# Causal attention and a recurrence taken in pieces of four batches amid the context attention before them

## The chip, the core and the metric

The kernel runs on one NeuronCore of a Trainium2 chip, in fp32, as one program with hand-placed work on TensorE (PE in the profile; its weight loads, which can overlap its matmuls, are PEld), VectorE (DVE), ScalarE (ACT) and GpSimd (POOL). SyncE (SP) issues most transfers. The metric is the device time of one execution in microseconds (us); a median of several is compared with a median of several.

## The reference

A model of four layers works on `x`, 16 batches of 64 tokens with 256 features (1024 tokens in all). Each layer adds three blocks to `x`: an attention over a context of 16 x 1024 keys with 192 features, a token mixer, and an FFN. Each block is fed a layer norm of `x`.

```python
x = x + _L0_xattn_ref(_layernorm(x), ctx_768, ctx_768, ...)
x = x + _L0_attn_ref(_layernorm(x), ...)
x = x + _L0_ffn_ref(_layernorm(x), ...)
...
x = x + _L2_xattn_ref(_layernorm(x), ctx_768, ...)
x = x + _L2_attn_ref(_layernorm(x), ...)
x = x + _L2_ffn_ref(_layernorm(x), ...)
...
```

Three of them matter here. The mixer of layer 0 is a causal attention with 16 heads of 16 features within each batch's 64 tokens, with queries and keys RMS-normed over all 256 features:

```python
qkv = jnp.einsum('bglc,cd->bgld', xg, w_qkv)
q, k, v = jnp.split(qkv, 3, axis=-1)
q = rmsnorm(q, ln_w)
k = rmsnorm(k, ln_w)
...
att = jnp.einsum('bghqd,bghkd->bghqk', q, k) * scale
att = jax.nn.softmax(jnp.where(causal, att, -jnp.finfo(att.dtype).max), axis=-1)
y = jnp.einsum('bghqk,bghkd->bghqd', att, v)
...
return jnp.einsum('btc,cd->btd', y, w_proj)
```

The FFN of layer 0 is a mixture of 8 experts: a gate's softmax chooses two per token, and a shared SwiGLU with 384 hidden features is added for all tokens. The mixer of layer 2 is a linear recurrence over a batch's 64 tokens with 128 complex states:

```python
Bu = jnp.einsum('hd,bld->blh', B_norm, x)
_, h = jax.lax.associative_scan(_binop, (Lam, Bu), axis=1)   # h_t = Lam * h_(t-1) + Bu_t
y = jnp.einsum('oh,blh->blo', C, h).real + D * x
```

All these blocks but the mixture's routing work on each batch by itself, so once the context attention has written the `x` of some batches, their mixer can begin.

## The kernel before, in words

`x` stays on chip as `xs`, 8 tiles of 128 tokens (two batches each; NT = 8). `LAYERS` names the blocks; `run` calls them in turn, each with its own SBUF pool (`lp`) and PSUM pools (`lps`, and the shared `misc` buffers, two in most blocks). Weights come through `ring`, two slots of 7296 columns; `slot` takes the next, `load` issues one weight's DMA on SP, and `pack` hands a block its weights and starts the loads of the block after it.

**Order.** Each engine executes its instructions in the order in which they were built. By default a scheduler orders PE's; within `manual_schedule` PE's order is the order in which the program text is run. A tile's PSUM or SBUF buffer is given out again when its last reader is done, so a producer may wait for the reader of an older tile.

**Layer 0's context attention** (`L0_xattn`, L269). The key projection is folded into the queries (`qp`), so scores come directly from the fetched context. `staggered` runs `first` (L293) for step i and then `second` (L307) for step i - 1, eight steps of two batches. `first` fetches the context of two batches (`fetch_ctx`, two layouts, 3.07 MB a step in all), makes scores of 128 queries x 1024 keys in PSUM tile `sc` (two buffers) and takes maximum (DVE) and exponential (ACT) in `exp_rows` (L218). `second` transposes probabilities (`keys_first`, L226; one copy out of PSUM by DVE, one by ACT), averages the context, transposes the average, projects it and adds it to `xs`.

**The causal attention** (`L0_attn`, L544). It starts with a DMA that writes zeros to `hs`, the 3.4 MB array in HBM that holds the experts' tokens. `norm_x` norms all 1024 tokens and transposes them to `hT`. A first loop over the 8 tiles computes q, k and v, scales q and k by their RMS (`nhalf` is the exponent of a POOL power), transposes them and spreads them by heads into `qs` and `kT`. The second loop takes groups of four batches and half the heads of each as steps: scores of 64x64 blocks (L596), mask, maximum, exponential, sums (DVE, POOL, ACT); transposes (`turned`, L629), averages (L642), division by the sums (`shares`, `weighed`, L658 to L669) and projection (L686). Two or three steps are in flight at a time, in an order written out by hand.

**Layer 0's FFN** (`L0_ffn`, L993). `norm_x`, then `gate_logits`, `gate_softmax` (L926; its first DVE instruction is `g_mx`), `two_largest`, `ranks`, `blocks`, `slots_of` compute on DVE to which row of `hs` each token goes. `scatter` (L1104) writes the tokens there with 16 indirect DMAs on POOL. Expert weights are gathered by indirect DMAs (`L0_block`, L966). `swiglu` (L973) computes the shared part in two halves of 512 tokens: hidden features from PSUM tiles tagged `gu`, silu on ACT, a product on DVE into `hid`, output product, add to `xs`. PE gets it after the gate. Then 23 blocks of 128 rows: read tokens from `hs` (`hb`, on SP), gated product, output to `ys`.

**Layer 2** (`heads64`, L358, then `L2_attn`, L1433). `heads64` is an attention with 8 heads of 64 features, also used in layer 3, with PE's order by hand. In its loop it calls `breathe()` four times a step and `finished(i)` when the tile i of `xs` is complete. In layer 3 these hooks run pieces of that layer's mixer (`state_space`, whose `go` is the hook at L1760) between the pieces of attention; in layer 2 they do nothing. `with_keys` (L409) makes the folded queries `qp` in PSUM tiles that DVE copies out. `L2_attn` norms all tokens, then takes two halves of 512 tokens: two products with B, a rotation by cos and sin, two scans, a rotation back (14 elementwise instructions shared by DVE and POOL), the products with C, and an add to `xs`; `later_steps` makes the mask that restarts the scan at each batch.

Of the kernel before, what the change touches and what calls it, by code (L numbers as in the profile page):

```python
# [19 lines left out]
T = B * S  # L20
# [13 lines left out]
    "L0_xattn", "L0_attn", "L0_ffn", "L1_xattn", "L1_attn", "L1_ffn",  # L34
    "L2_xattn", "L2_attn", "L2_ffn", "L3",
# [5 lines left out]
class Net:  # L41
# [220 lines left out]
    def pack_L0_xattn(self):  # L262
        self.slot()
        return (
            self.load("L0x_WqT"), self.load("L0x_Wk"),
            self.load_ctx_weights("L0x_WvT", "L0x_bv"),
        )

    def L0_xattn(self):  # L269
        nc = self.nc  # L270
        wq, wk, wv = self.pack(ahead=False)
        self.more_ctx(self.lp)
        self.norm_x()
        hT = self.hT
        qT = self.lp.tile([128, 2, T], F32, name="qT")
        for half in range(2):
            cols = bass.ts(half, 512)
            for o in range(2):
                ps = self.misc([128, 512])
                self.mm(ps, [(wq[:, c, o * 128 : (o + 1) * 128], hT[:, c, cols]) for c in range(2)])  # L280
                nc.vector.tensor_scalar(
                    qT[:, o, cols], ps, self.col("L0x_bq", o), D**-0.5, ALU.add, ALU.mult
                )
        qp = self.lp.tile([HC + 1, 2, T], F32, name="qp")
        for half in range(2):
            cols = bass.ts(half, 512)
            for ch in range(2):
                rows = HC + ch
                ps = self.misc([rows, 512])
                self.mm(ps, [(wk[:, o, ch * HC : ch * HC + rows], qT[:, o, cols]) for o in range(2)])  # L290
                self.evict(qp[:rows, ch, cols], ps)

        def first(i):  # L293
            ctx = [self.fetch_ctx(2 * i + par) for par in range(2)]
            sc = self.lps.tile([128, KEYS], F32, tag="sc", bufs=2, name="sc")
            for kh in range(2):
                keys = bass.ts(kh, 512)
                for ch in range(2):
                    for par in range(2):
                        b = 2 * i + par  # L300
                        nc.tensor.matmul(
                            sc[64 * par : 64 * par + 64, keys], qp[: HC + ch, ch, b * S : (b + 1) * S],
                            ctx[par][0][: HC + ch, ch, keys], start=ch == 0, stop=ch == 1,
                        )
            return ctx, self.exp_rows(sc)

        def second(i, got):  # L307
            ctx, p = got
            pT = self.keys_first(p)
            o = self.misc([128, CD + 1])  # L310
            for t in range(NK):
                for par in range(2):
                    nc.tensor.matmul(
                        o[64 * par : 64 * par + 64, :], pT[:, t, 64 * par : 64 * par + 64], ctx[par][1][:, t, :],
                        start=t == 0, stop=t == NK - 1,
                    )
            on = self.averages(o, CD + 1)
            ps = self.misc([128, 2, 128])
            nc.tensor.transpose(ps[:HC, 0, :], on[:, :HC], self.ident)
            nc.tensor.transpose(ps[: HC + 1, 1, :], on[:, HC:], self.ident)  # L320
            onT = self.lp.tile([HC + 1, 2, 128], F32, tag="onT", bufs=2, name="onT")
            nc.vector.tensor_copy(onT[:HC, 0, :], ps[:HC, 0, :])
            nc.scalar.copy(onT[: HC + 1, 1, :], ps[: HC + 1, 1, :])
            po = self.misc([128, D])
            self.mm(po, [(onT[: HC + ch, ch, :], wv[: HC + ch, ch, :]) for ch in range(2)])
            self.add_to_x(i, po)


        self.staggered(first, second, range(NT))
        self.start_pack(self.at)  # L330
        del self.ctxT[2:], self.ctx[2:]
# [26 lines left out]
    def heads64(self, large=None, breathe=lambda: None, finished=lambda i: None):  # L358
# [111 lines left out]
        with self.tc.manual_schedule(engines={mybir.EngineType.PE}):  # L470
# [8 lines left out]
            for k in range(len(steps) + 2):  # L479
# [12 lines left out]
                breathe()  # L492
# [5 lines left out]
                breathe()  # L498
                if one is not None:
                    one["pT"].append(self.keys_first(one["p"][1]))  # L500
                breathe()
# [3 lines left out]
                breathe()  # L505
# [16 lines left out]
    def pair_masks(self):  # L522
# [3 lines left out]
        of = self.lp.tile([8, 2, 128], I32, name="of")  # L526
        nc.gpsimd.iota(of, pattern=[[128, 2], [1, 128]], base=0, channel_multiplier=0)
        nc.vector.tensor_scalar(of, of, 4, None, ALU.logical_shift_right)
        head = self.lp.tile([8, 2, 128], F32, name="head")
        nc.vector.tensor_copy(head, of)  # L530
        mine = self.lp.tile([8, 2], F32, name="mine")
        sel = self.lp.tile([8, 2, 2, 128], F32, name="sel")
# [3 lines left out]
        own = self.lp.tile([128, 2], F32, name="own")  # L536
# [3 lines left out]
    def pack_L0_attn(self):  # L540
        self.slot()
        return self.load("L0a_wqkv"), self.load("L0a_wproj")

    def L0_attn(self):  # L544
        nc = self.nc
        wqkv, wproj = self.pack()

        self.nc.sync.dma_start(
            self.hs.rearrange("(n p) d -> p n d", p=128),
            self.zero.unsqueeze(1).to_broadcast([128, SLOTS // 128, D]),  # L550
        )
        self.norm_x()
        hT = self.hT

        lw = self.lp.tile([128, 2, 2], F32, name="lw")
        for c in range(2):
            nc.vector.tensor_scalar(lw[:, c, :], self.pair4, self.col("L0a_lnw", c), None, ALU.mult)
        qs = self.lp.tile([128, 2, B, 2, S], F32, name="qs")
        kT = self.lp.tile([128, 2, T], F32, name="kT")
        v = self.lp.tile([128, NT, D], F32, name="v")  # L560
        sel, own = self.pair_masks()
        for i in range(NT):
            cols = slice(i * 128, (i + 1) * 128)
            ps = self.misc([128, 2, D])
            self.mm(ps.rearrange("p a b -> p (a b)"), [(hT[:, c, cols], wqkv[:, c, :512]) for c in range(2)])
            sq = self.lp.tile([128, D], F32, tag="sq", bufs=2, name="sq")
            ss = self.small.tile([128, 2], F32, name="ss")
            for j in range(2):
                nc.scalar.activation(sq, ps[:, j, :], AF.Square, accum_out=ss[:, j : j + 1])
            nc.vector.tensor_scalar(ss, ss, 1.0 / D, 1e-6, ALU.mult, ALU.add)  # L570
            rr = self.small.tile([128, 2], F32, name="rr")
            nc.gpsimd.tensor_tensor(rr, ss, self.nhalf.to_broadcast([128, 2]), ALU.pow)
            qk = self.lp.tile([128, 2, D], F32, tag="qk", bufs=2, name="qk")
            for j in range(2):
                nc.vector.tensor_scalar(qk[:, j, :], ps[:, j, :], rr[:, j : j + 1], None, ALU.mult)
            pv = self.misc([128, D])
            self.mm(pv, [(hT[:, c, cols], wqkv[:, c, 512:]) for c in range(2)])
            nc.scalar.copy(v[:, i, :], pv)
            pt = self.lps.tile([128, 2, 2, 128], F32, tag="t", bufs=2, name="pt")
            for j in range(2):  # L580
                for c in range(2):
                    nc.tensor.transpose(pt[:, j, c, :], qk[:, j, c * 128 : (c + 1) * 128], self.ident)
            for c in range(2):
                for h in range(2):
                    nc.vector.tensor_scalar(
                        qs[:, c, 2 * i : 2 * i + 2, h, :], pt[:, 0, c, :].rearrange("p (b s) -> p b s", s=S),
                        lw[:, c, h : h + 1], None, ALU.mult,
                    )
                nc.vector.tensor_scalar(kT[:, c, cols], pt[:, 1, c, :], self.col("L0a_lnw", c), None, ALU.mult)

        sums = {}

        def first(x):  # L596
            g, jp = x
            if not jp:
                sums[g] = self.lp.tile([128, 4, 8], F32, tag="sums", bufs=2, name="sums")
            sc = [self.lps.tile([128, 2, 4, S], F32, tag="sc", bufs=2, name="sc") for _ in range(2)]  # L600
            for c in range(2):
                for bl in range(4):
                    b = 4 * g + bl
                    for u in range(2):
                        rows = slice(64 * jp + 32 * u, 64 * jp + 32 * u + 32)
                        self.mm(
                            sc[u][:, c, bl, :],
                            [(qs[rows, c, b].rearrange("p h q -> p (h q)"), kT[rows, c, b * S : (b + 1) * S])],
                        )
            ps = []  # L610
            for u in range(2):
# [12 lines left out]
                ps.append(p)  # L624
            return ps

        os = {}

        def turned(x, p):  # L629
            pT = []  # L630
# [1454 lines left out]
```

## Time and profile before

| | |
|---|---|
| median of 3 runs | 3145.02 us (3143.34 to 3146.72) |
| profiled execution | 3149.47 us, its span 3147.7 us |
| mean granted clock of TensorE | 0.928 |
| busy: PE, DVE, ACT, POOL | 2778.8 us (88%), 1476.1 (47%), 995.2 (32%), 309.9 (10%) |
| instructions | 42539 |
| moved by DMA | 273.17 MB, 87 GB/s on average |

The stages that the change touches, by the trace, in us from the span's start:

| stage | from | to |
|---|---|---|
| layer 0: context attention (first scores to last output) | 31.5 | 145.3 |
| layer 0: causal attention, norm, gate logits | 146 | 286.8 |
| layer 0: routing, shared FFN, scatters | 286.8 | 334.5 |
| layer 0: expert blocks | 334.5 | 546 |
| layer 2: context attention | 1430 | 1943.6 |
| layer 2: recurrence (last product) | 1943.6 | 1982.5 |

The rows of a page's second part cut the span in 40 slices of 78.7 us. A digit is the busy share in tenths (9 is 90% or more); PEclk is the clock that TensorE was granted, in tenths of full speed. In finer windows that clock takes two values in this trace, 1.00 and 0.50, and a matmul record takes twice as long at the lower. The profile's PE records are modelled at their ends, so a PE that counts as busy is not at its peak.

A line of the timeline gives start, duration, engine, line, operation, output<-inputs, shape and number of instructions in a run, and in brackets the idle time before it with what ended it. L65 is the line of the helper `mm`, so most matmuls carry it and are told apart by the output's name.

### The profile page before, as it was taken

The page shows a single profiled execution, that of the slowest core. Times are in us where ns is not written, and L with a number is a line of the kernel's source. Part 1 is how long each engine was busy: PE and PEld are TensorE (multiplying, and loading weights), DVE is VectorE, ACT ScalarE, POOL GpSimd, SP SyncE. Part 2 cuts the span into 40 slices and gives each one's busy share as a digit, 9 for nine tenths or more (in the row PEclk, how much of TensorE's full clock was granted, in tenths as well). Part 3 has the DMA queues.
Part 4 walks back from the last instruction along what each step waited for, and adds up shares of the span by engine and source line. Part 5 has one row for each costly group of instructions (what it writes and reads, how often), then busy time and mean ns, then how long its engine had stood idle before and what let it go on. Part 6 is the DMA issues. An engine that isn't in the chain of part 4 may idle for free.

```text
span 3147.7 us, 42539 instructions
## 1 busy us (share of the span) xinstructions
PE 2778.8 (88%) x16960; PEld 2001.5 (64%) x16960; DVE 1476.1 (47%) x2992; ACT 995.2 (32%) x2126; POOL 309.9 (10%) x417
## 2 busy tenths in 40 slices
PE   7889799699999879788999998496999888887899
PEld 3466688366666536685777776495676666665668
DVE  3365111566666672224344434322344756657591
ACT  1121121255555411122223322021324545455330
POOL 1022221300000020321000001302000000000000
PEclk8977899799999988798999999697999999998999
DMA  9701775210010100761111211364112212121110
GB/s 258 197 1 52 276 272 193 64 31 32 21 31 21 48 1 27 259 223 37 51 51 41 61 51 41 117 219 147 51 41 79 76 41 88 41 78 57 51 38 7
DMA packets 149408, 273.17 MB, mean 87 GB/s; under 512 B 16511, under 2 KB 103258, under 8 KB 142426
## 3 DMA queue, kind: packets, MB, share of 16 engines
q1 hardware_dynamic: 127418, 170.90, 18.1%
q0 software_dynamic: 14784, 93.26, 8.2%
q10 hardware_dynamic: 7008, 6.29, 0.6%
q8 instruction: 133, 2.18, 0.3%
q14 instruction: 65, 0.53, 0.1%
HBM read 247.83 MB, written 20.45 MB: 85 GB/s over the span
## 4 chain that ended last, share of the span: by engine, by line
PE 70%; DVE 12%; issue 6%; ACT 4%; DMA 3%; POOL 3%; SPq 1%; ACTq 0%; DVEq 0%; POOLq 0%
PE misc L65 12%; PE sc L437 8%; PE halves L65 7%; PE gu L65 6%; PE po L65 4%; PE misc L233 4%; PE ps_h L65 4%; PE ps_t L233 3%; PE sc L65 3%; PE misc L776 2%; PE o L824 2%; DVE x L1725 2%; PE misc L790 2%; ACT p L223 2%; DVE nmx L221 2%
## 5 line engine op out<-in xcount | busy, mean ns | idle before, releaser
L221 DVE TENSOR_REDUCE nmx<-sc 128x1 f32<-128x1024 f32 x264 | 311.7, 1219 | 238.3 <-PE sc L437 150.9
L223 ACT ACTIVATE p<-sc,nmx 128x1024 f32<-128x1024 f32 x264 | 294.0, 1115 | 339.2 <-DVE nmx L221 338.2
L437 PE MATMUL sc<-ctxT,qp 128*128 128x512 f32 (+1 forms) x1024 | 355.5, 602 | 0.0
L437 PEld LDWEIGHTS sc<-ctxT,qp 128*128 128x128 f32 (+1 forms) x1024 | 138.4, 190 | 154.1 <-issue 153.7
L158 POOL TENSOR_TENSOR ln_rs<-ln_ve,nhalf 128x1 f32<-128x1 f32 x120 | 66.6, 560 | 1463.8 <-DVE ln_ve L156 1377.0
L65 PE MATMUL halves<-ctx,pT 128*128 128x193 f32 x1024 | 187.6, 337 | 9.2 <-DVE xs L85 4.1
L65 PEld LDWEIGHTS halves<-ctx,pT 128*128 128x128 f32 x1024 | 175.6, 198 | 12.0 <-DVE xs L85 4.6
L65 PE MATMUL misc<-ctx,pT 128*128 128x193 f32 x1024 | 179.0, 327 | 0.2 <-DVE qT L402 0.2
L233 PE MATMUL ps_t<-ident,p 128*128 128x128 f32 x1088 | 151.2, 282 | 24.1 <-ACT p L223 20.2
L65 PEld LDWEIGHTS misc<-ctx,pT 128*128 128x128 f32 x1024 | 167.8, 191 | 1.5 <-issue 0.8
L233 PEld LDWEIGHTS ps_t<-ident,p 128*128 128x128 f32 x1088 | 129.4, 145 | 46.9 <-ACT p L223 26.1
L1725 DVE TENSOR_TENSOR_SCAN x<-da,x 128x512 f32<-128x512 f32 x128 | 152.3, 1214 | 2.1 <-ACT da L1715 1.4
L1715 ACT ACTIVATE da<-rep,al 128x252 f32<-128x252 f32 x256 | 114.7, 498 | 111.6 <-DVE x L1725 91.5
L233 PE MATMUL misc<-ident,p 128*128 128x128 f32 x1024 | 138.2, 281 | 7.0 <-ACT p L223 6.7
L235 ACT COPY pT<-ps_t 128x512 f32<-128x512 f32 x174 | 99.5, 582 | 134.6 <-PE ps_t L233 134.2
L65 PE MATMUL gu<-dT,wa 128*128 128x128 f32 (+1 forms) x1104 | 134.4, 281 | 4.0 <-issue 3.5
L65 PEld LDWEIGHTS gu<-dT,wa 128*128 128x128 f32 (+1 forms) x1104 | 126.6, 186 | 12.7 <-ACT yb L1142 6.3
L233 PEld LDWEIGHTS misc<-ident,p 128*128 128x128 f32 x1024 | 111.6, 142 | 32.7 <-ACT p L223 13.5
L65 PE MATMUL po<-wb,hid 128*128 128x256 f32 x516 | 124.5, 388 | 0.0
L65 PE MATMUL ps_h<-r,w 128*128 128x256 f32 x512 | 115.3, 385 | 0.0
L237 DVE COPY pT<-misc 128x512 f32<-128x512 f32 x128 | 88.3, 690 | 43.5 <-PE misc L233 37.6
L65 PEld LDWEIGHTS ps_h<-r,w 128*128 128x128 f32 x512 | 97.8, 192 | 16.6 <-issue 2.9
(438 smaller groups left out, 4413.5 us busy)
## 6 DMA issues: line engine op xcount, KB each, us to landing
ctx<-in_ctx SPq DMA_DIRECT2D x48, 768.0 KB
ctxT<-in_ctxT SPq DMA_DIRECT2D x48, 512.0 KB
w<-in_L2f_W SPq DMA_DIRECT2D x24, 1024.0 KB
rep<-dus SPq DMA_DIRECT2D x256, 64.0 KB
ctxT<-in_ctxT SPq DMA_DIRECT2D x16, 768.0 KB
ctxT<-in_ctxT SPq DMA_DIRECT2D x96, 128.0 KB
hb<-hs SPq DMA_DIRECT2D x46, 128.0 KB
ys<-yb ACTq DMA_DIRECT2D x46, 128.0 KB
```

The costliest lines, as they stand in the source:

```text
L65: self.nc.tensor.matmul(out, lhsT, rhs, start=n == 0, stop=n == len(pairs) - 1)
L158: nc.gpsimd.tensor_tensor(rs, ve, self.nhalf, ALU.pow)
L221: self.nc.vector.tensor_reduce(nmx, sc, AX.X, ALU.max, negate=True)
L223: self.nc.scalar.activation(p, sc, AF.Exp, bias=nmx, accum_out=sums)
L233: self.nc.tensor.transpose(ps[:, u, :], p[:, at : at + 128], self.ident)
L235: self.nc.scalar.copy(pT[:, 4 * g : 4 * g + 4, :], ps)
L237: self.nc.vector.tensor_copy(pT[:, 0:4, :], ps)
L437: nc.tensor.matmul(sc[u][:, bass.ts(kh, 512)], qp[n][par][rows, h : h + 2, :].rearrange("p h q -> p (h q)"), ctx[0][rows, at], start=n == ...
L776: nc.tensor.matmul(ps[kh], wk[:, kh, cols], cT[:, bass.ts(kh, 512)], start=True, stop=False)
L790: nc.tensor.matmul(ps[kh][:, u, :], cT[:, 512 * kh + at : 512 * kh + at + 128], wv[:, 0, :], start=u == 0, stop=False,)
L1715: nc.scalar.activation(da[:, g, :, 1:], now[j][:, 0, :].rearrange("p (b s) -> p b s", s=S)[:, :, 1:], AF.Exp, scale=al[:, col : col + 1],)
L1725: nc.vector.tensor_tensor_scan(flat, da.rearrange("p g b s -> p (g b s)"), flat, 0.0, ALU.mult, ALU.add)
```

## The change

The blocks `L0_xattn` and `L0_attn`, and of `L0_ffn` the norm and the gate's product, become one block `L0_first`. The blocks `L2_xattn` and `L2_attn` become `L2_xattn_attn`.

In both, the mixer is written as a generator that works on a chunk of 256 tokens (four batches, two tiles of `xs`; NC = 4 chunks) and yields between its pieces. `go` runs one piece: it starts chunk k once the context attention has finished tiles up to 2k + 1. At any time at most one chunk is open.

**L0_first.** Seven calls of `attn.go()` lie in each step of the context attention, at fixed places in PE's order by hand. The loop is:

```diff
+            held = tail = None
+            for n in range(NT + 2):
+                got = (n, *scores(n)) if n < NT else None
+                attn.go()
+                if tail is not None:
+                    onT = by_features(tail[1])
+                attn.go()
+                if held is not None:
+                    i, ctx, p = held
+                    pT = self.keys_first(p)
+                if tail is not None:
+                    output(tail[0], onT)
+                    attn.ready = tail[0] + 1
+                attn.go()
+                attn.go()
+                tail = None
+                if held is not None:
+                    tail = i, averaged(i, ctx, pT)
+                attn.go()
+                attn.go()
+                attn.go()
+                held = got
+                if n == NT - 1:
+
+                    nc.sync.dma_start(
+                        self.hs.rearrange("(n p) d -> p n d", p=128),
+                        self.zero.unsqueeze(1).to_broadcast([128, SLOTS // 128, D]),
+                    )
+            del self.ctxT[2:], self.ctx[2:]
+            shared = self.swiglu(
+                *self.shared, 384, self.add_to_x, 0, lambda: self.lps.tile([128, 512], F32, tag="t", bufs=2, name="gu")
+            )
+            while attn.go() and attn.done < NT // 2:
+                pass
+            while attn.go():
+                next(shared, None)
+            for _ in shared:
+                pass
+        self.spare_dve = False
```

So a step's output is one step later than before (`scores(n)`, `keys_first` of n - 1, `output` of n - 2). The weights of the causal attention, the gate and the shared FFN are loaded after the first two context fetches; the DMA that zeroes `hs` moves to the end of the context fetches. `sc` has one buffer instead of two, and both attentions share it. With `spare_dve` the copies out of PSUM that alternated between DVE and ACT go to ACT alone. The room for `qs`, `kT`, `v`, normed q and k, probabilities and their transposes is taken from the weight ring's second slot (`pack_L0_room`); the rest lies in a second pool `sb`.

**A chunk of the causal attention** computes what `L0_attn` did for four batches, as one chain. Its pieces are separated by `yield`:

```diff
+        def chunk(g):
...
+                mv, rs = self.norm_tile(x, 1e-5)
+                os.append(sb.tile([128, D], F32, tag="os", bufs=2, name="os"))
+                nc.vector.tensor_scalar(os[t], x, mv[:, 0:1], rs, ALU.subtract, ALU.mult)
+            yield
...
+                self.evict(hT[:, :, t * 128 : (t + 1) * 128], self.transposed(os[t]))
+            yield
+            for t in range(2):
...
+                self.mm(ps.rearrange("p a b -> p (a b)"), [(hT[:, c, cols], wqkv[:, c, :512]) for c in range(2)])
...
+                nc.scalar.copy(v[:, t, :], pv)
+                yield
+            for t in range(2):
+                pt = self.lps.tile([128, 2, 2, 128], F32, tag="t", bufs=2, name="pt")
...
+                yield
+            sums = sb.tile([128, 4, 8], F32, tag="sums", bufs=2, name="sums")
+            for jp in range(2):
+
+                sc = self.lps.tile([128, 2, 2, 4, S], F32, tag="sc", bufs=1, name="sc")
...
+                yield
...
+            yield
+            ps = self.misc([128, 2, E])
+            for t in range(2):
+                cols = slice((2 * g + t) * 128, (2 * g + t + 1) * 128)
+                self.mm(ps[:, t, :], [(self.hT[:, c, cols], self.gate_w[:, c, :]) for c in range(2)])
+            nc.vector.tensor_copy(self.logits[:, 2 * g : 2 * g + 2, :], ps)
+            s.done = g + 1
+            yield
+
+        def go():
+            if s.work is None and s.next < NC and s.ready >= 2 * s.next + 2:
+                s.work = chunk(s.next)
+                s.next += 1
+            if s.work is not None and next(s.work, s) is s:
+                s.work = None
+            return s.work is not None or s.next < NC
```

In the part left out are the transposes of the probabilities, averages, division, projection, the add to `xs`, the second norm into `htok` and `hT`, as before.

**The shared SwiGLU** becomes a generator for one half. Half 0 is built in `L0_first`, half 1 in `L0_ffn`, where the gate's softmax now reads stored logits:

```diff
-    def swiglu(self, w1, w3, w2, hidden, add):
+    def swiglu(self, w1, w3, w2, hidden, add, half, room):
...
     def L0_ffn(self):
         nc = self.nc
-        gw, sw1, sw3, sw2 = self.pack()
-        self.norm_x()
-        p = self.gate_softmax(self.gate_logits(gw))
+        p = self.gate_softmax(self.logits)
...
-        self.swiglu(sw1, sw3, sw2, 384, self.add_to_x)
+        for _ in self.swiglu(
+            *self.shared, 384, self.add_to_x, 1, lambda: self.lps.tile([128, 512], F32, tag="gu", bufs=4, name="gu")
+        ):
+            pass
+        self.start_pack(self.at)
```

**L2_xattn_attn.** `recurrence` has the setup of `L2_attn` and a generator of chunks, in five pieces with PE work or elementwise work; tiles of 256 columns stand where those of 512 stood. Its `go` is called by `heads64`, which passes the place of the call, and skips place 3:

```diff
-    def heads64(self, large=None, breathe=lambda: None, finished=lambda i: None):
+    def heads64(self, large=None, breathe=lambda place: None, finished=lambda i: None):
...
-                breathe()
+                breathe(0)
...
+    def L2_xattn_attn(self):
+
+
+        with self.tc.manual_schedule(engines={mybir.EngineType.PE}):
+            lru = self.recurrence()
+            self.heads64(breathe=lru.go, finished=lru.more)
+            self.start_pack(self.at)
+            while lru.go():
+                pass
...
+            bu = []
+            for n, m in enumerate((br, bi)):
+                ps = self.misc([128, CHUNK])
+                self.mm(ps, [(m[:, c, :], hT[:, c, :]) for c in range(2)])
                 u = tmp(f"bu{n}")
-                nc.scalar.activation(flat(u), flat(ps), AF.Copy, scale=gamma)
+                nc.scalar.activation(flat(u), ps, AF.Copy, scale=gamma)
                 bu.append(u)
+            yield
...
+        def go(place=0):
+            if place == 3:
+                return
```

The order of the elementwise instructions within a chunk is that of a half before; each is half as wide, and there are twice as many.

## The prediction

> **What bounds the kernel now.** The page's slice rows come first: TensorE (PE) is busy in nearly every slice, so time is lost where it waits or where its granted clock (PEclk) is low. The slices that the change touches are 0 to 4 (78.7 us each) and 24 and 25.
>
> ```profile
> PE   7889799699999879788999998496999888887899
> PEclk8977899799999988798999999697999999998999
> ```
>
> Then busy time by stage (columns: window, its length, busy us of PE, weight loads, DVE, ACT, POOL, clock, DMA share, GB/s), cut at the stages' ends:
>
> ```profile
> 31.00:60.00 29.00, 22.43 (x134) 11.32 (x134) 8.51 (x20) 4.32 (x7) 1.10 (x2) 0.88 1.08 306
> 60.00:146.00 86.00, 70.14 (x369) 35.59 (x366) 24.41 (x58) 11.78 (x18) 3.08 (x6) 0.86 0.85 217
> 146.00:287.00 141.00, 121.36 (x821) 87.55 (x821) 85.31 (x222) 30.46 (x75) 26.89 (x33) 0.73 0.06 20
> 287.00:334.00 47.00, 31.50 (x102) 18.30 (x101) 15.61 (x64) 4.90 (x8) 21.52 (x22) 0.84 0.43 151
> 1880.00:1930.00 50.00, 49.77 (x260) 37.08 (x259) 20.22 (x45) 14.45 (x32) 2.00 (x3) 1.00 0.21 64
> 1943.00:1983.00 40.00, 22.62 (x67) 13.95 (x65) 29.89 (x59) 4.24 (x8) 18.17 (x16) 0.74 0.00 0
> ```
>
> Up to 146 is layer 0's attention over the context: DMA carries it, PE waits little. From 146 to 287 is the causal attention, norm and gate: PE busy 86%, but at 0.73 clock. To 334 the routing runs; PE works off the shared FFN and then idles. In the third block the context attention fills PE (1880 to 1930: 99%, clock 1.00), while the recurrence after it (1943 to 1983) runs on VectorE and POOL.
>
> The timeline of PE shows how the clock is lost (start, us, instructions, in brackets the idle time before and its releaser):
>
> ```profile
> 217.31 2.00 PE L65 MATMUL sc<-kT,qs 32*128 32x64 f32 x32
> 219.24 1.09 PE L635 MATMUL pt<-ident,p 128*128 128x128 f32 x8
> 223.62 1.79 PE L653 MATMUL o<-p16T,v 64*32 64x128 f32 x32 [3.29 <-DVE p16T L58]
> ```
>
> The same 32 score records take 2.00 us here, but 3.67 us at 192.5 and 201.2. After the idle 3.29 us the clock is 0.50 until about 241, where the next dense product restores it. In two-microsecond windows it is 0.50 over 186 to 217, 224 to 241, 248 to 265 and 272 to 282: 75 us that do half their work, **37 us lost**.
>
> Routing is a chain across engines that starts as the gate's logits stand:
>
> ```profile
> 286.95 0.22 DVE L923 TENSOR_REDUCE g_mx<-misc 128x8 f32<-128x64 f32 x1 [4.13 <-PE misc L65]
> 300.38 1.20 POOL L1124 DMA_INDIRECT wa<-in_L0f_w,rows  x1 [21.34 <-PE po L65]
> 321.05 0.97 POOL L1108 DMA_INDIRECT hs<-htok,s_at  x1 [0.30 <-DMA hs<-htok,s_at]
> 334.46 0.44 PE L65 MATMUL gu<-dT,wa 128*128 128x128 f32 x1
> ```
>
> 13.4 us of VectorE, 16 scatters at 1.27 us, then token reads: 47.5 us to the first expert product. Both halves of the shared FFN (280 to 317) lie hidden beside it.
>
> **First block, part by part.** *Start.* The 3.4 MB zero-fill, issued at 29.6, leaves the early DMA stream; 2.2 MB of attention and FFN weights enter it. Step 2's keys then need 11.7 MB, at 245 GB/s (the 50 to 70 us window) 48 us, against 58.2 now; step 3 comes 12.5 us later (3.07 MB). One score buffer instead of two makes step 1 wait for step 0's reduce and exp (1.22 + 1.11 + hand-overs = 2.8 us), hidden by that data. Step 3, where chunk 0 enters, starts at about **60**.
>
> *PE work from there, at full clock.* Context attention: 5 scores at 3.6 (32 records in 7.11), 6 times transposes 1.1 plus averages 2.85, 7 outputs at 1.55: 53 us. One chunk of four batches: norm transposes 0.66; qkv 5.2 (512-column records at 0.43 us, 256-column at 0.215); q/k transposes 1.2; scores 2 x 2.0; p transposes 2 x 1.09; averages 2 x 1.5; shares 0.6 + 2.0; projection 1.8; second norm's transposes 0.66 and gate 0.9: 22.2. Four chunks 89. Sum **142**.
>
> *Waits inside the chunks.* Before, two groups were in flight. Now a chunk is one chain whose filler is context work, and PE's order is fixed. From row durations with 0.1 to 0.2 us per hand-over: residual add 0.42, stats 0.43 + 0.17 + 0.14, POOL power 0.55, scaling 0.41 = 2.9 us ahead of norm transposes; q/k scaling before the second qkv tile gets its PSUM buffer 3.0 (two squares at 0.58, 0.17, POOL 0.70, two scalings at 0.48, less the v product); the shared score buffer, or six evictions at 0.34, 2 to 2.6; masking before the second score group up to 1.6 where nothing lies between; transposed probabilities 0.8; weighing 1.2. By what stands between in PE's built order: chunks 0 to 2 about 10, 9 and 9. Chunk 3 starts after the last context output and runs alone: 15. With small evictions **46**.
>
> *Clock.* Such waits of 2 to 3 us recur twice a step. [...] 2.40 us of idle before 185.9, followed by transposes, put the clock at 0.50 within 2 us and kept it there until 217; at that rate 37 are lost, as now (total +10). The nearest row for work so mixed is layer 3, where pieces of a recurrence already lie amid a context attention with waits of 2 us:
>
> ```profile
> 2450.00:2550.00 100.00, 86.34 (x463) 60.49 (x461) 68.30 (x105) 47.69 (x116) 1.79 (x3) 0.93 0.20 60
> 2550.00:2650.00 100.00, 89.87 (x487) 65.12 (x486) 52.85 (x85) 49.83 (x107) 3.49 (x7) 0.97 0.23 69
> 2650.00:2750.00 100.00, 84.98 (x456) 61.52 (x454) 69.60 (x113) 46.46 (x117) 1.70 (x3) 0.95 0.20 59
> ```
>
> The dense context products bring the clock back each time: 0.95. I take that for the mixed part (53 + three chunks at 22.2 + waits 31 = 151 us, over 0.95: 8 lost), and 0.73, the causal attention's own, for chunk 3 alone (22 + 15 = 37, over 0.73: 14 lost): **22 us**. Ends 5 and 55.
>
> Logits stand at 60 + 142 + 46 + 22 = **270**, against 287 now: 17 us gained.
>
> *The gate behind the shared FFN.* While chunk 3 is unfinished, `attn.done < NT // 2` (four) holds, so no shared piece runs amid the attention; half 0 follows it. In VectorE's built order the three `hid` products and four residual adds of half 0 stand between the logits' copy and `g_mx`. VectorE executes in order, so routing waits for half 0: gate and up 12 matmuls x 0.85 = 10.2, last product 0.9, down 12 x 0.43 = 5.1, add 0.6, and half clock at the start 1 to 2: **+18 us**. Now that distance is nothing. Half 1 still hides beside routing, so moving half 0 earlier saves nothing.
>
> *Queues.* On SP, nine loads for layer 1 (2.7 MB, 11 us) now stand ahead of the 23 token reads, the first five waiting until half 1 frees the ring. The 20 us of scatters hide them; without that cover 11 us. Four of them used to run at 327 to 334 beside the first expert gathers; that contention goes: -2 (0 to -4). The zero-fill falls late in the stream, ahead of its users. Copies moved from DVE to ACT (0.58 for 0.68) lie beside other pieces; ACT is 22% busy there.
>
> First block: -17 + 18 - 2 = **-1 us**.
>
> **Third block.** Now 39.0 us run from the last context output (1943.6) to PE's last recurrence product (1982.5). Three of four chunks move inside. The fourth stays after it: add 0.6, norm 2.4, transposes and copy 1.0, products 1.7, scaling 0.5, the elementwise chain half of 14.4 = 7.2, output 1.9: 15.3, **saving 23.7**. Inside, PE is full: each chunk adds 0.7 + 1.7 + 1.7 = 4.1, three **+12.3**. The ten VectorE instructions of a chunk stand in one block ahead of the copies that free `with_keys`' PSUM buffers: 8.5 to 9.3 us after `bu`, while PE comes for a buffer after 3.6 + 1.16 + 1.89 = 6.65. That is 2.6 us a chunk, **+8** (0 to 15: VectorE products beside POOL take 1.69 instead of 0.69). Expert weights follow the freed slot as now. Sum **-4** (-12 to +4).
>
> **Total** -5. The profiled execution took 3149.5 us (span 3147.7), the three runs' median is 3145.0; the difference goes on the median: **3140**.
>
> **Rivals.** (A, 0.45) As summed; own range -25 to +15 (3120 to 3160) by waits and clock. (B, 0.22) The waits are half what I count, 26 instead of 46, because the row durations overlap more than a chain added end to end says: -25, 3120 (-45 to -7). For it: from 150 to 184, with two groups in flight, PE had small gaps alone. Against: here one chunk is in flight. (C, 0.23) The clock goes as in the causal attention now: 37 lost instead of 22, and VectorE's block in the third block makes 15 instead of 8: -5 + 15 + 7 = +17, 3162 (+6 to +40). For it: 2.40 us sufficed at 185.9, and what follows a wait here is often transposes and 64-row records. It decides from about 11 us, one half-clock stretch of 22 us more than A's. (D, 0.10) The gate's delay is no cost, because the expert start is set by reads and gathers: -5 - 18 = -23, 3122. Against: scatters need the slots that routing computes. That the change doesn't interleave as said holds for the shared FFN and is in the sum.
>
> About 0.2%, 6.3 us, is what a measurement here tells from no change. Faster: 0.20 of A, 0.21 of B, 0.09 of D, 0.50. Same: 0.18 of A, 0.05 of the others, 0.23. Slower: 0.07 of A and 0.20 of C, 0.27. The range reaches just past B's centre and C's: 3116 to 3164.
>
> **What would show it.** `g_mx` at about 288 (A), 268 (B), 303 (C); 17 to 19 us between the logits' copy and `g_mx`, else that step is wrong; the clock between 60 and 270 near 0.9 (A) or 0.83 (C); PE idle ahead of second qkv tiles and norm transposes of about 3 us; first expert product 47 us after `g_mx`, else the queue step fails; in the third block PE waits of 2 to 3 us a chunk and about 15 us of tail. A first expert product before 310 would refute the forecast on the fast side, one after 355 on the slow side.

## The result, and the profile after

| | before | changed |
|---|---|---|
| median, 6 runs each on the same chips | 3145.8 us (3142.15 to 3149.18) | 3130.42 us (3127.12 to 3137.05) |
| profiled execution | 3149.47 us | 3130.54 us |

The changed kernel takes 0.9946 of the time before (95% interval 0.9928 to 0.9964): **15.4 us faster**, where 5 were forecast. The two profiled executions differ by 18.9 us, because the one of before lies 4 us above its median. Legs of the two traces are compared below with that in mind.

The slice rows of the changed kernel's page (78.2 us a slice):

```profile
PE   6887899699999879788999999496999888887899
PEclk9897899799999988799999999698999999998999
```

Rows this coarse hardly tell the two apart: the clock has a tenth more in slice 0, two more in slice 2 and one less in slice 1. Gains of 0.5% have to be read from the stages. Busy time by stage of the changed kernel (window, length, busy us of PE, weight loads, DVE, ACT, POOL, then clock, DMA share, GB/s), cut at its own stage ends (last logits 265.1, g_mx 283.7, first expert product 327.6, recurrence 1948 to 1966):

```profile
60.00:146.00 86.00, 74.58 (x492) 47.66 (x490) 39.38 (x105) 23.55 (x54) 10.22 (x14) 0.88 0.74 210
146.00:266.00 120.00, 96.48 (x734) 69.34 (x733) 61.19 (x159) 28.09 (x64) 20.66 (x26) 0.82 0.13 39
266.00:284.00 18.00, 18.00 (x51) 9.90 (x50) 3.97 (x10) 3.07 (x4) 0.00 (x0) 0.90 0.00 0
284.00:328.00 44.00, 17.55 (x60) 10.24 (x59) 11.79 (x56) 3.53 (x6) 21.54 (x22) 0.73 0.49 178
1880.00:1930.00 50.00, 49.84 (x260) 36.80 (x256) 21.01 (x44) 15.42 (x31) 2.00 (x3) 1.00 0.21 64
1948.00:1966.00 18.00, 8.49 (x24) 5.53 (x22) 14.40 (x46) 1.32 (x3) 8.62 (x13) 0.72 0.01 1
```

(The second to the fourth row have no counterpart of equal length before: there 146 to 287 and 287 to 334 stood for them.) The causal attention's work now starts before 100 us, so the stretch to the logits ends at 265 and not at 287. But 266 to 284 is new: PE is full with the FFN's half 0 while VectorE, POOL and DMA are nearly idle. The timeline of VectorE in this stretch shows why that costs:

```profile
265.13 0.17 DVE L763 COPY logits<-misc 128x16 f32<-128x16 f32 x1 [2.29 <-PE misc L65]
271.08 0.69 DVE L1048 TENSOR_TENSOR hid<-g,gu 128x512 f32<-128x512 f32 x1 [5.78 <-PE gu L65]
274.52 0.69 DVE L1048 TENSOR_TENSOR hid<-g,gu 128x512 f32<-128x512 f32 x1 [2.75 <-PE gu L65]
277.95 0.69 DVE L1048 TENSOR_TENSOR hid<-g,gu 128x512 f32<-128x512 f32 x1 [2.75 <-PE gu L65]
279.43 0.42 DVE L85 TENSOR_TENSOR xs<-xs,misc 128x256 f32<-128x256 f32 x1 [0.79 <-PE misc L65]
...
283.33 0.42 DVE L85 TENSOR_TENSOR xs<-xs,misc 128x256 f32<-128x256 f32 x1 [0.88 <-PE misc L65]
283.67 0.21 DVE L991 TENSOR_REDUCE g_mx<-logits 128x8 f32<-128x64 f32 x1
```

The logits stand at 265.3, and `g_mx`, which needs nothing else, comes 18.5 us later, behind three products and four adds that wait for PE in turn.

Where the two traces part (us from each span's start):

| milestone | before | changed | lead | gained in the leg |
|---|---|---|---|---|
| last logits of layer 0 (`g_mx` before) | 286.95 | 265.1 | -21.8 | 21.8 |
| `g_mx` | 286.95 | 283.7 | -3.3 | -18.6 |
| first expert product | 334.5 | 327.6 | -6.9 | 3.6 |
| layer 2's first scores | 1435.3 | 1424.9 | -10.4 | 3.5 |
| its last context output | 1943.6 | 1948.2 | +4.7 | -15.0 |
| last recurrence product | 1982.5 | 1965.2 | -17.4 | 22.0 |
| layer 2's `g_mx` | 2000.3 | 1980.0 | -20.3 | 2.9 |
| end of span | 3147.7 | 3128.8 | -18.9 | -1.4 |

The 3.5 us between the first expert product and layer 2 need no cause of their own: from that product to layer 1's gate the profiled executions of this study took anything from 913.4 to 919.4 us, though none of the kernels changes TensorE's work there.

In the third block the context attention grew and its tail shrank. Its windows from first scores to last output, first of the kernel before, then of the changed one:

```profile
1435.00:1944.00 509.00, 500.19 (x2721) 368.23 (x2719) 202.43 (x435) 151.07 (x322) 18.19 (x27) 0.99 0.17 50
```

```profile
1424.00:1948.00 524.00, 510.97 (x2784) 377.64 (x2783) 222.44 (x480) 155.44 (x331) 30.30 (x41) 1.00 0.17 49
```

The 63 matmuls more are about what three chunks bring (20 each); PE stays 98% busy. After it, by the timeline of PE in the changed kernel, only the last chunk is left:

```profile
1948.06 0.38 PE L177 MATMUL misc<-ident,os 128*128 128x128 f32 x2
1951.26 0.44 PE L177 MATMUL misc<-ident,os 128*128 128x128 f32 x2 [2.81 <-DVE ln_ve L156]
1952.16 3.52 PE L65 MATMUL misc<-hTs,w 128*128 128x256 f32 x8 [0.46 <-ACT hTs L60]
1961.39 1.19 PE L65 MATMUL misc<-w,ur 128*128 128x256 f32 x2 [5.72 <-DVE ur L1607]
```

The norm of its second tile (2.81 us of waiting) and the elementwise chain (5.72) are what PE waits for.

### The profile page after: what moved, and what is told of

The parts are those of the page before. It is cut to its first block, busy times and chain, and to the rows that moved or that the text cites. A ratio compares the mean times of both kernels' runs of the same rounds, so it can differ in the third digit from the quotient of the medians.

```text
span 3128.8 us, 42567 instructions
## 1 busy us (share of the span) xinstructions
PE 2750.3 (88%) x16976; PEld 1987.6 (64%) x16976; DVE 1463.2 (47%) x2986; ACT 1010.6 (32%) x2160; POOL 310.5 (10%) x425
## 3 DMA queue, kind: packets, MB, share of 16 engines
q1 hardware_dynamic: 127418, 170.90, 18.6%
## 4 chain that ended last, share of the span: by engine, by line
PE 65%; DVE 10%; issue 7%; ACT 4%; DMA 3%; POOL 2%; SPq 1%; ACTq 0%; DVEq 0%; POOLq 0%
PE misc L65 10%; PE sc L498 8%; PE halves L65 7%; PE gu L65 6%; PE po L65 4%; PE misc L233 4%; PE ps_h L65 4%; PE ps_t L233 3%; PE sc L65 2%; PE misc L844 2%; PE o L892 2%; PE misc L858 2%; DVE x L1832 2%; ACT p L223 2%; PE misc L177 2%
```

## The experiments

Every kernel was timed beside the kernel before. Ratios are to that one; the changed kernel's own is 0.9946.

**The two blocks apart.** e1 keeps only the first block's change, e2 only the third's.

```diff
 # e1: LAYERS, and with it L2_attn of before
-    "L2_xattn_attn", "L2_ffn", "L3",
+    "L2_xattn", "L2_attn", "L2_ffn", "L3",
 # e2, on the kernel before, with recurrence and heads64 of the changed kernel
-    "L2_xattn", "L2_attn", "L2_ffn", "L3",
+    "L2_xattn_attn", "L2_ffn", "L3",
```

> Only the first block is changed; layer 2 runs as before. By the milestones of the two traces (first expert product 6.9 us earlier, end of the expert blocks 7.7, layer 2's first scores 10.4): 8 to 10 us faster than before, ratio 0.997. If the whole gain were the third block's, it would be within 2 us of before; if the first block's two gains and its loss are as the forecast had them (-1 us), 1 us faster.

> Only the third block is changed; layer 0 runs as before. By the traces the context attention of layer 2 grew by 15.0 us and what follows it up to the gate shrank by 24.9: 9 to 10 us faster, ratio 0.997. The forecast's sum for this part was 4 us faster (stalls of 8 us). If the two parts hinder each other, e1 and e2 together give more than the whole change's 15 us.

e1 took 3134.77 us against 3145.78, ratio 0.9959 (0.9944 to 0.9975): 11.0 us faster. e2 took 3137.61, ratio 0.9966 (0.9954 to 0.9978): 8.2 us faster. Both parts gain. Their sum, 19, agrees with the whole change's 15 within the intervals, so nothing speaks for an interplay.

**The gate ahead of the shared FFN.** e3 takes half 0 out of `L0_first` and runs both halves behind the routing's text, as the kernel before did.

```diff
-            shared = self.swiglu(
-                *self.shared, 384, self.add_to_x, 0, lambda: self.lps.tile([128, 512], F32, tag="t", bufs=2, name="gu")
-            )
-            while attn.go() and attn.done < NT // 2:
-                pass
             while attn.go():
-                next(shared, None)
-            for _ in shared:
                 pass
...
-        for _ in self.swiglu(
-            *self.shared, 384, self.add_to_x, 1, lambda: self.lps.tile([128, 512], F32, tag="gu", bufs=4, name="gu")
-        ):
-            pass
+        for half in range(2):
+            for _ in self.swiglu(
+                *self.shared, 384, self.add_to_x, half,
+                lambda: self.lps.tile([128, 512], F32, tag="gu", bufs=4, name="gu"),
+            ):
+                pass
```

> The changed kernel with half 0 of the shared FFN moved behind the gate again, so that both halves run beside the routing. Theory (the gate waits for half 0 on VectorE, 18.6 us between the logits' copy and g_mx): g_mx within 1 us of the last logits, first expert product at about 310 instead of 327.6, 16 to 18 us faster than the changed kernel, ratio to before about 0.989. Rival (expert start is set by gathers, scatters and reads, or by TensorE that must still work off both halves): first expert product stays after 322, less than 5 us gained.

e3 took 3114.32 us, ratio 0.9891 (0.9875 to 0.9907), 16 us below the changed kernel. Its timeline of VectorE:

```profile
262.88 0.17 DVE L756 COPY logits<-misc 128x16 f32<-128x16 f32 x1 [1.59 <-PE misc L65]
263.09 0.22 DVE L984 TENSOR_REDUCE g_mx<-logits 128x8 f32<-128x64 f32 x1
```

`g_mx` follows the copy at once, and the first expert product comes at 307.6 instead of 327.6. Both FFN halves still end (290) before TensorE gets the first tokens to transpose (303). So the 18.6 us were on the path, and what hides the FFN is the routing.

**Half 0 amid the last chunk.** e4 changes one number, so that half 0's pieces alternate with those of chunk 3.

```diff
-            while attn.go() and attn.done < NT // 2:
+            while attn.go() and attn.done < NC - 1:
```

> The changed kernel with half 0's seven pieces amid the last chunk of the causal attention (attn.done < NC - 1). Now 222 to 284 us holds this chunk alone and then half 0: 62 us for some 38 us of work at full clock. Theory (the last chunk loses about 10 us to waits without a filler and 11 us to a clock of 0.70, both of which dense FFN products fill): both are done in 46 to 50 us, g_mx at 268 to 272, 12 to 16 us faster than the changed kernel. Rival (the filler delays the chunk as much as it fills, since the two share PSUM buffers and VectorE): less than 5 us gained.

e4 took 3116.44 us, ratio 0.9897 (0.9881 to 0.9913), 14 us below the changed kernel. The windows of chunk 3, first of the changed kernel (without half 0), then of e4 (with it):

```profile
222.00:266.00 44.00, 33.99 (x204) 23.27 (x203) 19.35 (x49) 9.92 (x23) 6.65 (x8) 0.69 0.11 34
```

```profile
224.00:273.00 49.00, 42.43 (x257) 27.26 (x257) 23.54 (x61) 13.02 (x27) 6.75 (x9) 0.92 0.09 30
```

For 5 us more, e4 does 16 us more of work, counted at full clock: idle time fell from 10.0 to 6.6 us, and the clock went from 0.69 to 0.92. Summed over windows of 2 us, busy time times what the clock lacks of 1 is 11.7 us lost in the changed kernel and 3.8 in e4.

**The added loads.** e5 issues layer 1's nine loads after the fourth block's token read.

```diff
-        self.start_pack(self.at)
...
             dT = self.block_tokens(j)
+            if j == 4:
+                self.start_pack(self.at)
```

> The changed kernel with layer 1's nine weight loads issued after the fourth expert block's token read instead of ahead of the first. g_mx to the first expert product is 43.9 us in the changed kernel and 47.5 before. Theory (in the kernel before, four of these loads ran at 327 to 334 us beside the first expert gathers; in the changed one they are done by 307): here they run beside later gathers, the first expert product still comes 43 to 44 us after g_mx, and the time is within 3 us of the changed kernel. Rival (having them ahead of the token reads costs the queue, which the scatters only hide in part): first product 1 to 3 us sooner than in the changed kernel.

3129.5 us, ratio 0.9944 (0.9928 to 0.996). `g_mx` to the first product took 43.9 us (281.0 to 324.9), exactly as in the changed kernel. That they stand ahead of the token reads costs nothing; the 3.6 us gained in this leg fit their absence from 327 to 334, which e5 keeps.

**The zero-fill.** e6 moves it in the kernel before; e11 moves it back in the changed kernel.

```diff
 # e6, on the kernel before: in first(i), and gone from L0_attn
             ctx = [self.fetch_ctx(2 * i + par) for par in range(2)]
+            if i == NT - 1:
+                self.nc.sync.dma_start(
+                    self.hs.rearrange("(n p) d -> p n d", p=128),
+                    self.zero.unsqueeze(1).to_broadcast([128, SLOTS // 128, D]),
+                )
 # e11, on the changed kernel: the same DMA, gone from n == NT - 1
             ctxs = {i: fetch(i) for i in range(2)}
+            nc.sync.dma_start(
...
```

> The kernel before with only one thing changed: the zero-fill of hs is issued with the last context fetch of layer 0. Theory (the first block's gain is the clock: 60 us to the last logits lost 45.6 us of clock in the kernel before, 29.3 in the changed one, with idle time equal at 35): moving the 3.4 MB brings the transfers of the second step forward by 4 to 5 us, but the causal attention after it is as it was, so 3 to 8 us faster than before. Rival (the whole gain of the first block, 11 us, is this transfer, 3.4 MB at some 260 GB/s being 13 us): 10 to 13 us faster, as e1.

> The changed kernel with the zero-fill of hs back after the first two context fetches. Theory (the gain of the first block is part transfer, part clock: the late zero-fill alone gave the kernel before 4 to 5 us of the 11): the third step's keys come up to 13 us later, chunk 0 starts 4 to 10 us later, and the time is 4 to 8 us above the changed kernel. Rival (with the chunks in between, TensorE needs 20 us a step and the context stream catches up): within 2 us of the changed kernel, and the whole gain of the first block is the interleaving's.

e6 took 3139.94 us against 3145.04, ratio 0.9988 (0.9978 to 0.9997): some 4 to 5 us faster. In its trace `g_mx` came 10.3 us before that of the kernel before (286.95):

```profile
276.63 0.22 DVE L924 TENSOR_REDUCE g_mx<-misc 128x8 f32<-128x64 f32 x1 [4.13 <-PE misc L65]
```

e11 took 3142.04 against 3149.1, ratio 0.9981 (0.9968 to 0.9994): about 11 us of the changed kernel's gain are gone, more than the 4 to 8 expected. The timeline of PE in e11 shows the price:

```profile
63.16 1.94 PE L328 MATMUL sc<-ctxT,qp 96*64 96x512 f32 x2 [13.07 <-DMA ctxT<-in_ctxT]
70.26 6.21 PE L328 MATMUL sc<-ctxT,qp 96*64 96x512 f32 x14 [5.15 <-DMA ctxT<-in_ctxT]
```

and the same two groups in the changed kernel:

```profile
50.84 1.55 PE L324 MATMUL sc<-ctxT,qp 96*64 96x512 f32 x2 [4.24 <-DMA ctxT<-in_ctxT]
53.87 5.72 PE L324 MATMUL sc<-ctxT,qp 96*64 96x512 f32 x14 [1.47 <-DMA ctxT<-in_ctxT]
```

In e11 step 2's scores end 17 us later, the last logits 14 us later (279.1), `g_mx` 13.9 us later. So most of what the early transfers lose, the end loses. In e11 the fill and the 2.2 MB of weights both stand ahead of step 2; the kernel before had only the fill there. That may be why e6 gained less; it is not shown, for the two intervals (1 to 7 us for e6) do not part the two effects.

**The recurrence's block.** e7 cuts the elementwise block in two.

```diff
             nc.vector.tensor_tensor(ui, ui, t2, ALU.subtract)
+            yield
...
-            for _ in range(2):
-                yield
+            yield
```

> The changed kernel with the recurrence's block of elementwise instructions cut in two pieces by a yield (in place of one of the two empty pieces). In the trace of the changed kernel TensorE waits 1.7, 2.4 and 0.5 us more in the three chunks that lie inside the context attention. Theory (VectorE's block ahead of the copies of with_keys): these waits shrink by half, 2 us faster, not to be told from noise. Rival (they come from the first pieces of a chunk, norm and transposes): unchanged.

3130.15 us, ratio 0.9948 (0.9931 to 0.9966): no change. PE's idle time between 1436 and 1936 us is the same to 0.1 us (7.7), with the same waits at the same places. The theory that they come from this block falls. The longest, 0.90 us at a transpose of the normed tile in each of the first two chunks and 0.75 at a context average in the second, stand before the elementwise block is issued.

**Filling the waits.** e8 and e9 add matmuls that nobody reads, ahead of the waiting ones in chunk 3; e9 has half as many.

```diff
+        def fill(g, n=2):
+            if g == NC - 1:
+                for _ in range(n):
+                    nc.tensor.matmul(self.misc([128, 512]), self.ident, wqkv[:, 0, :512], start=True, stop=True)
...
             for t in range(2):
                 pt = self.lps.tile([128, 2, 2, 128], F32, tag="t", bufs=2, name="pt")
+                if t:
+                    fill(g)
...
                 sc = self.lps.tile([128, 2, 2, 4, S], F32, tag="sc", bufs=1, name="sc")
+                fill(g)
...
```

Further calls stand ahead of the second half of the probabilities' transposes, the projection and the transposes of `htok` (there with twice the number).

> The changed kernel with 14 matmuls of 128x512 added whose products nobody reads (0.43 us each at full clock, 6 us in all), placed where TensorE waits in the last chunk of the causal attention (222 to 265 us: 10.0 us idle, clock 0.70, 11.7 us lost). Theory (the clock falls because of the waits of 0.9 to 2.1 us between small products, and dense work in them holds it): this stretch shrinks from 43 to 33 to 37 us, g_mx at 275 to 279, 5 to 9 us faster than the changed kernel. Rival (the clock falls with the small products themselves, whatever lies in the waits): clock stays near 0.7 in this stretch, and the time is the same or up to 6 us slower.

> As e8 with half the added matmuls: 7, which are 14 records of some 0.45 us at full clock, 6.3 us (e8's 14 were 28 records, 12.6 us, not the 6 expected; there the stretch's idle time fell from 10.0 to 3.7 us, its clock rose from 0.70 to 0.84, and its length stayed). Theory (the clock follows the waits): clock about 0.80 again, and the stretch 3 to 6 us shorter than the changed kernel's, g_mx at 278 to 281. Rival (only work that fills nearly all the time holds the clock): clock below 0.75, stretch as long as before or longer.

e8 took 3131.22 us, ratio 0.9957 (0.9944 to 0.9969): no gain. e9 took 3125.21 against 3146.67, ratio 0.9927 (0.9914 to 0.9941), 5 us below the changed kernel, with the intervals overlapping at their edges. The window of chunk 3 in e9:

```profile
222.00:266.00 44.00, 40.40 (x231) 24.25 (x232) 19.80 (x51) 10.56 (x24) 6.66 (x8) 0.83 0.10 34
```

The clock rose from 0.69 to 0.83 by 6.3 us of work that is of no use. What that is worth in time stays open. From chunk 2's gate product, up to which the kernels are alike, to `g_mx` the changed kernel took 64.0 us (219.7 to 283.7), e8 59.6 and e9 57.6. But e1, e5 and e7, whose text in this stretch is the changed kernel's, took 60.9, 65.7 and 60.8, so single executions scatter by 5 us here, and e9 lies only 3 us below the least of them. The gate product itself came anywhere from 215.3 to 224.8 us in nine kernels with the same text up to it.

**Both together.** e10 is e3 with four of these matmuls.

```diff
 # on e3: fill(g, n=1) ahead of the second q/k transposes, both score groups, the second p transposes
```

> e3 (half 0 behind the gate) with 4 such matmuls, ahead of the second q/k transposes, both groups of scores and the second half of the probabilities' transposes in the last chunk. If e9's theory holds, g_mx 2 to 4 us before e3's 263, so 2 to 4 us faster than e3, ratio to before 0.988; by the rival the same as e3 or 2 us slower.

e10 took 3110.8 us, ratio 0.9875 (0.9858 to 0.9893), the fastest of all: 20 us below the changed kernel. Against e3 (0.9891) the 3.5 us are not resolved. Its `g_mx` came at 267.5, not before 263, because its chunk 2 ended late; from that chunk's gate product to `g_mx` it took 42.9 us, e3 46.8, a difference within that scatter.

## Why the prediction was right, and where its terms were off

The direction held, and the time lies in A's own range. But the gain was three times the forecast, 3130 lies midway between A's centre (3140) and B's (3120), and a range of 48 us is hard to miss. Of the mechanism, the gate's delay and the work moved under the context attention are shown. Rival D is refuted by e3. Between A, B and C the counts below do not choose: the waits (35.0 us) came nearer to B's 26 than to A's 46, and the clock's loss (29.3) lies midway between A's 22 and C's 37.

**First block.** Measured over windows of 2 us from 60 to 266 us in the changed kernel:

| term | forecast | measured |
|---|---|---|
| first scores of step 3 | about 60 | 66.0 |
| work at full clock from 60 us | 142 | 141.7 (171.0 busy less 29.3 lost) |
| waits, chunks 0 to 2 and chunk 3 | 31 + 15 = 46 | 24.9 + 10.0 = 35.0 |
| clock, mixed part and chunk 3 | 8 + 14 = 22 | 17.6 + 11.7 = 29.3 |
| last logits | 270 | 265.1 |

Waits were counted too high and the clock's loss too low; that the errors nearly cancel is luck. So is part of the fit of the work: at 60 us seven sets of averages and eight outputs were still to come, not six and seven.

One wait was most of the error. Ahead of the second qkv tile the forecast had 3.0 us, for the q/k scaling that frees a PSUM buffer. In the trace PE waits there 0.47 us in each of the four chunks, for the copy of `v` (L649) alone; four times 2.5 us is 10 of the 11 us.

```profile
85.31 2.85 PE L65 MATMUL misc<-w,hTs 128*128 128x512 f32 x8 [0.47 <-ACT w L649]
```

The mixed part ran at 0.88, not at layer 3's 0.95. A chunk of the causal attention brings groups of 32x64 and 64x128 matmuls with waits between; that this is the reason was not tested. Measured the same way, the kernel before lost 45.6 us to the clock and 35.5 to idle time between 60 and 288 (e2, with the same text there, 42.2 and 37.4). So interleaving cut no idle time; it gained 13 to 16 us of clock. About 5 us more of the lead lie in busy time. Some 2 of them are shared-FFN products that the kernel before ran ahead of its last logits; the rest stays open. The late zero-fill alone does not bring the clock's gain: e6 still lost 41.8 us to it up to its logits. Yet e6's `g_mx` came 10.3 us early, so in these traces about half of the lead at the logits is the fill's; by the medians the fill alone is worth 4 to 5 us.

*The zero-fill* was in the forecast as a part of the start: step 2's keys at 48 us instead of 58.2. The 14 score records that wait for them came at 53.9, and at 70.3 with the fill early (e11). It carries the first block: e11, the whole change without the late fill, is 7 us faster than before (2 to 10 by its interval), and e2's third block alone is worth 8 (7 to 14). So the interleaving with the gate's delay, but without the early start, comes to about nothing, give or take 5 us. By e3 the delay takes 16 us; then the interleaving itself brings about as much.

*The gate behind the shared FFN*: forecast +18, measured 18.6, and shown by e3 to be on the path. *Queues*: forecast -2, measured -3.6; e5 agrees that having the loads ahead of the token reads costs nothing.

At the first expert product the lead was forecast at 1 us and is 6.9: 5 from the logits, 1.6 from the queues, less 0.6.

**Third block.** Forecast 4 us gained; e2 measured 8.2 and the traces show 9.9. The context stage grew by 15.0 us. The added work was nearly right: 12.9 us at full clock, 12.3 forecast. The term that was off is the stalls: 8 forecast, and idle time between first scores and last output grew by 4.2 us (8.8 to 13.0). The forecast put them behind VectorE's block of ten; e7 shows that they don't come from it. The clock gave 2.1 us back (3.5 lost before, 1.4 after), all at the stage's start, which the sum did not have. The tail measured 16.9 us against 15.3. The gate gained 2.9 us that the sum did not have: VectorE scales six of the next norm's eight tiles (`htok`) from 1952.6 to 1962.7, within the tail, since those tiles of `xs` are complete. Before, all eight came at 1978.3 to 1987.5, about the end of the recurrence.

What would have refuted the forecast did not occur: `g_mx` at 283.7 (forecast 288), the first product at 327.6, 43.9 us after it (forecast 47). But three of the signs that it named for A failed. The clock between 60 and 270 us was 0.84, where 0.9 was to speak for A and 0.83 for C. PE waited 0.47 and not 3 us ahead of second qkv tiles; ahead of the first norm's transposes it waited 2.30 us in chunk 0 and at most 0.46 after. And the three chunks within layer 2's context attention did not wait 2 to 3 us each: idle time grew by 4.2 us in all.

Open: which piece of the chunk causes the remaining waits in layer 2, and how much of the 3.6 us in the routing leg is the loads alone, were not tried.

## What to carry to other kernels

When a block is cut up and moved into another, look at what the cutting put ahead of the next critical chain on each engine: here seven VectorE instructions of a product that had been hidden cost about as much as the whole interleaving brought (`g_mx` 18.6 us after the logits), and moving them back gave 16 us (e3). Work that can hide anywhere belongs beside the longest wait of the other engines (the routing, 16 us gained in e3) or in the gaps of a chain that has no filler of its own (14 us in e4), not between the two. A transfer that nobody needs for long goes to the end of a stream that feeds the start (issued early it took 11 us of the gain in e11, issued late it gave 4 to 5 in e6).

## What the runs showed of the hardware

The clock fell amid short waits: no idle gap of PE between 60 and 285 us of the changed kernel was longer than 2.30 us, and yet 29 us were lost. The timeline of PE shows one case: a wait of 1.69 us, and the second group of 32 score records takes 3.68 us where 2.00 is its time at full clock.

```profile
94.69 2.87 PE L65 MATMUL sc<-w 32*128 32x64 f32 x32 [1.69 <-ACT p L223]
...
101.09 3.68 PE L65 MATMUL sc<-w 32*128 32x64 f32 x32
104.69 1.97 PE L698 MATMUL pt<-ident,w 128*128 128x128 f32 x8
106.59 4.13 PE L334 MATMUL misc<-ctx,pT 128*64 128x193 f32 x32
110.66 1.08 PE L720 MATMUL o<-w 64*32 64x128 f32 x32
```

By 110.66, behind the averages (106.59), the clock is back: in windows of 2 us it is 0.50 from 96 to 108, 0.68 to 110 and then 1.00. In the last chunk the same small products ran at 0.69 alone, and at 0.83 and 0.92 with dense work in the gaps (e9, e4). Cut at the chunk's own ends, five traces without such work (changed kernel, e1, e5, e7, e11) had 0.65 to 0.75 there, so the rise is more than scatter. Whether it counts that a gap is closed or that dense work lies beside the small products, these runs do not separate.

A 128x512 fp32 product counted as two records of some 0.45 us here (e8's 14 as 28, eight of them in 3.60 us at 262.76), so it cost 0.9 us, not 0.43: e8's filler was twice as long as meant, 12.6 us, and its time is the changed kernel's.
